# Row numbers read in place, a tangent for the experts' weights, and one load of all weights copied by VectorE in the tail of a convolution, attention and mixture-of-experts kernel

## The chip, the cores and the metric

The kernel runs on one core of a Trainium2 chip. The time is the device time of one execution, in microseconds (us). The engines are PE (TensorE; PEld is its weight load), DVE (VectorE), ACT (ScalarE), POOL (GpSimd) and SP (SyncE, which here only issues DMAs). The sixteen DMA engines of the core are shared by all queues. PE, DVE and ACT run in an order that the program writes out; SP's and POOL's orders are made by the scheduler when the kernel is built.

## The reference

```python
# x: (8, 56, 56, 256), float32
h = relu(bn(einsum('nhwc,cd->nhwd', x, w1)));  h = relu(bn(conv3x3(h, w2)))   # 32 paths, 4 channels each
h = relu(bn(einsum('nhwd,dc->nhwc', h, w3)))
x = relu(sum over the 32 paths of h + x)
t = tokens(x)                                          # (8, 3136, 256)
u = layernorm(t);  k = v = headwise_layernorm(u)       # 8 heads of 32
t = t + u + u @ (k^T v / N)                            # linear attention, per image and head
u = layernorm(t)
p = softmax(u @ router_w.T);  w, e = top_k(p, 2);  w = w / w.sum()
t = t + u + sum over the two e of w_e * (gelu(u @ w1[e] + b1[e]) @ w2[e] + b2[e])   # 8 experts
```

With two experts chosen of which the logits differ by d, the weights w are 1 / (1 + exp(d)) and exp(d) / (1 + exp(d)).

## The kernel before

The 25088 tokens are cut into 56 chunks of 448 (7 chunks an image). The program has 65 slots. Slot s works on several chunks at once: the third convolution of chunk s, the first two of chunks s + 2 and s + 1, the end of chunk s - 1 (sum, transposes, norms, the image's key-value products), the attention of chunk s - 8, and the routing of chunks whose attention is done. Into this the tiles of the experts are mixed. From slot 57 on there is no convolution left: this, with the tiles that follow slot 64, is the tail. It begins near 2660 us.

- Routing (`route_steps`, groups of two chunks or one): the logits, the two best experts, `q` = the difference of their logits. POOL raises e to the power q (L1110, `ebase` holds e), DVE makes the two weights from it with an add and a reciprocal (L1148 to L1154) and writes them, with the token's number, into the three last columns of its row (`pay`, 259 wide). A matmul with a triangle (L1119, L1125) ranks the tokens of an expert; the rank plus `count` (L1131), plus the first row of the expert, `offs` (L1135), is the row in DRAM (`regions`). POOL scatters 112 rows with one indirect DMA (L1165).
- Planning (`plan_steps`, L1227 to L1322): after certain chunks, `count` tells how many full tiles of 256 rows each expert has; a table holds the first row and the expert of every tile.
- Tiles (`moe_steps`, 210 of them, each one expert and 256 rows): `take_rows` reads the row number from the table into a register of SP and loads 256 rows (L1359, 259 KB); `take_weights` does the same with the expert and loads its weights (`w`, 513 KB, L1369) from `Wd` in DRAM; `tile_in` transposes the rows (L1380, `te`) and copies the tokens' numbers into a small tile `index` (L1389; for the 30 tiles that may be partial L1392 and L1393 mask them first); `tile_mid` is the first product (L1420) and the gelu (L1424), `tile_out` the second (L1436, L1440) and the scaling (L1444, into `y`); `tile_add` lets POOL add 128 rows of `y` to the output in DRAM with an indirect DMA (L1458, two a tile, 420 in all). Step n of the loop holds the first stage of tile n, the middle of tile n - 1, the last of tile n - 2, the loads of rows n + 2 and of weights n + 1.
- Buffers: `rows` 5, `w` 4, `index` 6, `y` 4. A buffer of `y` and of `index` comes free when the add that reads it has landed.
- Adds are ordered by block: a token's two experts are handled in two halves of a round (`blocks`), and the first add of a half waits until all adds of the half before have landed.
- The end of a chunk: DVE adds the paths' sum, the bias and the input (L688) into a buffer `u`; ACT applies relu (L717); it is stored (L722) and transposed (L729), and the transposed copy is stored (L734). In the convolution, DVE splits `h2` into `hi` (L343) and `lo` (L344), which are spread by DMA (L350).

Of the kernel before, what the change touches and what calls it, by code (L numbers as in the profile page):

```python
# [8 lines left out]
F32 = mybir.dt.float32  # L9
# [16 lines left out]
def kernel(  # L26
# [68 lines left out]
    xtp = ctx.enter_context(tc.tile_pool(name="xtp", bufs=4))  # L95
    taps = ctx.enter_context(tc.tile_pool(name="taps", bufs=1))
    split = ctx.enter_context(tc.tile_pool(name="split", bufs=1))
    hlp = ctx.enter_context(tc.tile_pool(name="hlp", bufs=2))
# [34 lines left out]
    ebase = const.tile([P, 2 * KT], F32, name="ebase")  # L133
    nc.gpsimd.memset(ebase, 2.718281828459045)
# [183 lines left out]
    def conv2_steps(s):  # L318
# [19 lines left out]
        def halves():  # L338

            h2 = h2s[s]  # L340
            hi = split.tile([P, CH], F32R, tag="hi", name=f"hi_{s}")
            lo = split.tile([P, CH], F32R, tag="lo", name=f"lo_{s}")
            nc.vector.tensor_copy(hi, h2)  # L343
            ins = nc.vector.tensor_tensor(lo, h2, hi.bitcast(F32), ALU.subtract).ins  # L344
            if s == 0:
                halved.append(ins)
            hl = hlp.tile([P, NQ, CH], F32R, tag="hl", name=f"hl_{s}")
            for v, part in enumerate((hi, lo, hi, lo)):
                queue = nc.scalar if s == 0 and v % 2 else nc.sync
                queue.dma_start(out=hl[v : P : 4, :, :].bitcast(F32), in_=part.bitcast(F32))  # L350
            h2s[s] = hl
# [220 lines left out]
    offs = const.tile([P, M], F32, name="offs")  # L572
    code = const.tile([P, M], F32, name="code")
    for e in range(M):
        nc.gpsimd.memset(offs[:, e : e + 1], float(0 if e == 2 * E else e % E * CAPR + TR))
        nc.gpsimd.memset(code[:, e : e + 1], float(E - e % E))
# [18 lines left out]
    nc.vector.memset(count, 0.0)  # L595
    nc.vector.memset(taken, 0.0)
# [77 lines left out]
    def sum_paths(s, u):  # L674
# [10 lines left out]
        if ab == NQ - 1:  # L685
            if f == 0:
                usum[s] = one.tile([P, NF, CH], F32, tag="u", name=f"u_{s}")
# [373 lines left out]
    def route_steps(group):  # L1061
# [42 lines left out]
        def weights():  # L1104
# [5 lines left out]
            nc.gpsimd.tensor_tensor(q, ebase[:T, :K], q, ALU.pow)  # L1110
# [3 lines left out]
        def ranks():  # L1114
# [20 lines left out]
            nc.vector.tensor_add(at, at, offs[:T, None, None, :E].to_broadcast([T, K, 2, E]))  # L1135
# [9 lines left out]
        def rows():  # L1145
            q2 = v["q"]
            q1 = small([], "rq1")
            nc.vector.tensor_scalar_add(q1, q2, 1.0)  # L1148
            nc.vector.reciprocal(q1, q1)
            for n, m in enumerate(group):  # L1150
# [3 lines left out]
                nc.vector.tensor_mul(pay[:, :, C + 1], q2[:, mine], q1[:, mine])  # L1154
# [36 lines left out]
    def plan_steps(b):  # L1191
# [63 lines left out]
        def runs():  # L1255
# [10 lines left out]
            nc.vector.scalar_tensor_tensor(  # L1266
                start, start, float(TR), offs[:, None, :m].to_broadcast([P, 2, m]),
                op0=ALU.mult, op1=ALU.add
            )
# [60 lines left out]
    def entry(i, j, most):  # L1330
# [3 lines left out]
            place[0:1, j : j + 1], engines=[mybir.EngineType.SP],  # L1334
# [3 lines left out]
        if b not in landed:  # L1338
# [5 lines left out]
    def empty_rows(e):  # L1344
        pad = slots.tile([P, 2, ROW], F32, tag="rows", name=f"pad_{e}", bufs=5)
# [9 lines left out]
    def take_rows(i):  # L1355
        row = entry(i, 0, E * CAPR - TR)
        z = slots.tile([P, 2, ROW], F32, tag="rows", name=f"rows_{i}", bufs=5)
# [8 lines left out]
    def take_weights(i):  # L1366
        e = entry(i, 1, E - 1)
        w = slots.tile([P, WROW], F32, tag="w", name=f"w_{i}")
# [5 lines left out]
    def tile_in(i):  # L1374
# [11 lines left out]
        index = slots.tile([P, 2], I32, tag="index", name=f"index_{i}", bufs=6)  # L1386
        low = slot_of[i][3]
        if low is None:
            nc.vector.tensor_copy(index, z[:, :, C + 2].bitcast(I32))  # L1389
        else:  # L1390
# [4 lines left out]
            )  # L1395
        turned[i] = (eT, g, index)
# [49 lines left out]

    blocks = {}

    def tile_add():
# [5 lines left out]
        at = bass.IndirectOffsetOnAxis(ap=index[:, h : h + 1], axis=0)  # L1455
# [91 lines left out]
    for s in range(S + A + 1):  # L1547
# [56 lines left out]
        if s == S + 1:  # L1604
            apart.append(s)
# [63 lines left out]
```

## Time and profile before

| | |
|---|---|
| median of three runs | 3119.7 us (3117.6 to 3120.1) |
| profiled execution | 3117.4 us, of which the span of the profile is 3115.6 |
| PE busy | 2889.5 us, 93% |
| DVE busy | 2175.9 us, 70% |
| ACT busy | 1915.0 us, 61% |
| POOL busy | 1850.0 us, 59% |
| DMA | 537.5 MB, 173 GB/s over the span |
| weight loads (L1369) | 210 of 513 KB |
| adds (L1458) | 420, 1575 ns of POOL each |
| powers on POOL for the experts' weights (L1110) | 32, 52.9 us busy |
| index copies (L1389) | 180, 338 ns each |

The page of the profile divides the span into 40 slices and gives each engine's busy share in tenths, the clock that PE was granted and the share of the DMA engines. A row of a group reads: line, engine, operation, output and inputs, how many, busy time and mean duration, and the idle time of the engine before them with what ended it. Waits are inferred from semaphores; one for several things is put down to the last of them.

### The profile page before, as it was taken

Reading aid. Unit: us, or ns where it says so; the run is one execution under the profiler, and the core shown is the slowest. Engines: PE = TensorE matmul, PEld = TensorE weight load, DVE = VectorE, ACT = ScalarE, POOL = GpSimd, SP = SyncE. Lnnn points to the kernel's source line nnn. Section 1 sums busy time; section 2 is a strip of 40 time slices with the busy share of each in tenths; the row PEclk is TensorE's granted clock in tenths of the full one; section 3 lists DMA queues with packets and bytes.
Section 4 is the critical chain, followed back from the end, with each engine's and each line's share of the span. In section 5 each row is a group of like instructions: output and inputs, shape, how many; then the busy total and the mean of one; then the engine's idle time right before and its main releaser. Section 6 shows DMA issues by size and latency. Waiting matters only on the chain.

```text
span 3115.6 us, 53761 instructions
## 1 busy us (share of the span) xinstructions
PE 2889.5 (93%) x16677; PEld 1648.9 (53%) x16677; DVE 2175.9 (70%) x5743; ACT 1915.0 (61%) x3827; POOL 1850.0 (59%) x1375
## 2 busy tenths in 40 slices
PE   7999889888899999999999999999999997997898
PEld 3334434333455555555555555555555554776777
DVE  6778788788777887787877787787778885543100
ACT  4666566556666666667666666666666664554345
POOL 2332355445465766656766666676664656677677
PEclk9999999899999999999999999999999998998999
DMA  3434344435566767676766776767766666998897
GB/s 106 145 117 130 114 147 123 133 108 178 142 165 184 197 170 193 172 191 194 187 192 163 196 198 170 193 171 196 196 170 173 186 165 153 221 263 208 199 219 177
DMA packets 321710, 537.54 MB, mean 173 GB/s; under 512 B 40192, under 2 KB 231824, under 8 KB 321424
## 3 DMA queue, kind: packets, MB, share of 16 engines
q1 hardware_dynamic: 238464, 429.89, 45.1%
q0 software_dynamic: 82368, 103.47, 18.3%
q8 instruction: 133, 2.18, 0.3%
q14 instruction: 153, 1.25, 0.1%
q10 hardware_dynamic: 592, 0.76, 0.1%
HBM read 248.01 MB, written 192.55 MB: 141 GB/s over the span
## 4 chain that ended last, share of the span: by engine, by line
PE 70%; DVE 10%; ACT 6%; issue 5%; DMA 4%; POOL 4%; SPq 0%; POOLq 0%; DVEq 0%; ACTq 0%
PE c L660 14%; PE su L681 13%; PE ph L1420 10%; PE py L1440 8%; PE at L984 6%; PE c L326 4%; PE kv L830 3%; DVE r L668 3%; ACT r L665 3%; PE te L1380 3%; DMA out_dram<-y,index 2%; PE c L290 2%; PE py L1436 2%; POOL hsd L794 2%; PE tu L729 1%
## 5 line engine op out<-in xcount | busy, mean ns | idle before, releaser
L668 DVE SCALAR_TENSOR_TENSOR r<-c,nb,r 128x448 f32<-128x448 f32 x1792 | 1127.0, 676 | 378.8 <-ACT r L665 376.5
L665 ACT ACTIVATE r<-c,b3t 128x448 f32<-128x448 f32 x1792 | 1038.2, 634 | 347.1 <-PE c L660 343.2
L1458 POOL DMA_INDIRECT out_dram<-y,index x420 | 661.3, 1575 | 327.3 <-ACT y L1444 185.2
L660 PE MATMUL c<-hl,W3hl 64*128 64x448 f32 x3584 | 689.6, 428 | 32.3 <-ACT r L665 19.0
L1165 POOL DMA_INDIRECT regions<-pay,rrowi x448 | 428.4, 956 | 316.2 <-PE c L660 194.7
L660 PEld LDWEIGHTS c<-hl,W3hl 64*128 64x128 f32 x3584 | 325.6, 188 | 494.4 <-issue 208.7
L681 PE MATMUL su<-r,gather 128*32 128x448 f32 x3584 | 535.4, 564 | 38.4 <-DVE r L668 34.3
L1444 ACT ACTIVATE y<-py,rows 128x256 f32<-128x256 f32 x420 | 196.1, 475 | 465.7 <-PE py L1440 363.8
L1420 PE MATMUL ph<-eT,w 128*128 128x256 f32 x1680 | 451.6, 400 | 29.2 <-ACT hT L1424 10.7
L1440 PE MATMUL py<-w,hT 128*128 128x256 f32 x1680 | 433.1, 382 | 1.7 <-ACT hT L1424 1.7
L1420 PEld LDWEIGHTS ph<-eT,w 128*128 128x128 f32 x1680 | 299.3, 193 | 162.6 <-issue 34.6
L794 POOL TENSOR_TENSOR hsd<-hsd,half 112x36 f32<-112x36 f32 x49 | 302.6, 6175 | 87.6 <-DVE hsd L792 85.8
L1440 PEld LDWEIGHTS py<-w,hT 128*128 128x128 f32 x1680 | 292.1, 192 | 31.6 <-ACT hT L1424 2.1
L1424 ACT ACTIVATE hT<-ph,w 128x256 f32<-128x256 f32 x420 | 197.4, 479 | 173.2 <-PE ph L1420 116.7
L984 PE MATMUL at<-tab,tT 128*112 128x272 f32 x896 | 259.3, 413 | 9.7 <-ACT r L665 6.6
L755 POOL TENSOR_TENSOR norm<-t,hmean 112x512 f32<-112x512 f32 x112 | 117.1, 1085 | 212.9 <-ACT r L665 101.9
L681 PEld LDWEIGHTS su<-r,gather 128*32 128x32 f32 x3584 | 97.6, 109 | 223.4 <-DVE r L668 102.4
L1436 PE MATMUL py<-b2hl,own 128*128 128x256 f32 x420 | 182.0, 433 | 16.2 <-ACT lg L992 8.6
L984 PEld LDWEIGHTS at<-tab,tT 128*112 128x112 f32 x896 | 148.2, 179 | 84.3 <-issue 28.2
L1110 POOL TENSOR_TENSOR rq<-ebase,rq 112x8 f32<-112x8 f32 (+1 forms) x32 | 52.9, 1652 | 210.2 <-DVE rq L1109 209.2
L1436 PEld LDWEIGHTS py<-b2hl,own 128*128 128x128 f32 x420 | 80.2, 191 | 146.9 <-issue 47.6
L988 DVE SCALAR_TENSOR_TENSOR X<-at,rs,X 112x256 f32<-112x256 f32 x224 | 106.8, 477 | 68.0 <-PE at L984 67.7
(265 smaller groups left out, 3192.4 us busy)
## 6 DMA issues: line engine op xcount, KB each, us to landing
w<-Wd SPq DMA_DIRECT2D x210, 513.0 KB
rows<-regions SPq DMA_DIRECT2D x210, 259.0 KB
xi<-in_x_dram SPq DMA_DIRECT2D x56, 448.0 KB
hl<-hi SPq DMA_DIRECT2D x112, 224.0 KB
tTs<-u SPq DMA_DIRECT2D x56, 448.0 KB
ts<-t SPq DMA_DIRECT2D x56, 448.0 KB
tT<-tTs SPq DMA_DIRECT2D x56, 448.0 KB
X<-ts SPq DMA_DIRECT2D x56, 448.0 KB
```

Of the source, the lines that this page charges most:

```text
L660: product = nc.tensor.matmul(tiles[g][:, :CH], W3hl[rows, ab, cg, :], hl[rows, ab, :], start=True, stop=True)
L665: nc.scalar.activation(r, tiles[0][:, :CH], AF.Relu, bias=b3t[:, cg, 2 * ab : 2 * ab + 1])
L668: nc.vector.scalar_tensor_tensor(r, tiles[1][:, :CH], nb3[:, cg, 2 * ab + 1 : 2 * ab + 2], r, op0=ALU.max, op1=ALU.add,)
L681: nc.tensor.matmul(ps[32 * c4 : 32 * c4 + 32, :CH], gather, unit.pop((s, 4 * u + c4)), start=(ab == 0), stop=(ab == NQ - 1),)
L794: nc.gpsimd.tensor_tensor(sd, sd, half[:T, :].rearrange("q (k h) -> q k h", k=KT), ALU.pow)
L984: nc.tensor.matmul(ps, tT[:, f, k * T : (k + 1) * T], tables_of[b][:, f, :], start=(f == 0), stop=(f == NF - 1),)
L1165: ins = nc.gpsimd.indirect_dma_start(out=regions[n], out_offset=bass.IndirectOffsetOnAxis(ap=v["row_i"][:, (m - group[0]) * KT + k, n : n ...
L1420: nc.tensor.matmul(ps, w[:, f * C + hf * P : f * C + (hf + 1) * P], eT[:, f, :], start=(f == 0), stop=(f == NF - 1),)
L1424: nc.scalar.activation(hT[:, hf, :], ps, AF.Gelu, bias=w[:, 2 * NF * C + hf : 2 * NF * C + hf + 1])
L1436: nc.tensor.matmul(ps, own.to_broadcast([P, P]), b2hl, start=True, stop=False)
L1440: nc.tensor.matmul(ps, hT[:, f, h * P : (h + 1) * P], w[:, (NF + f) * C : (NF + f + 1) * C], start=False, stop=(f == NF - 1),)
L1458: ins = nc.gpsimd.indirect_dma_start(out=out_rows, out_offset=at, in_=y[:, h, :], in_offset=None, compute_op=ALU.add, **partial,).ins
```

## The change

Six things are changed together.

1. The token numbers are no longer copied for full tiles: the indirect DMA reads them in the row tile itself. The rows' buffers go from 5 to 8, and the `index` buffers of the partial tiles from 6 to 12.
2. `count` and `taken` start from the first rows of the experts, so that `offs` is added neither to each token's row nor to each plan.
3. The experts' weights come from tanh(q/2) on ACT, as 0.5 + 0.5 tanh and 0.5 - 0.5 tanh; the power on POOL and the reciprocal on DVE go.
4. When the convolution is over (slot 57), its buffers are given up, and in their place one DMA loads the weights of all eight experts (`experts`, 4.2 MB). From then on `take_weights` reads the expert's number into a register of DVE, and DVE copies 128x1026 numbers into `w`. That concerns 80 of the 210 tiles.
5. For the room, the convolution's pools lie on the other side of the memory, `lo` takes the place of `h2`, and the sum of the paths that of `xT` instead of `u`.
6. The memsets of `ebase` and of half of `offs` go.

```diff
-    xtp = ctx.enter_context(tc.tile_pool(name="xtp", bufs=4))
...
+    conv_pools = [
+        tc.tile_pool(name=name, bufs=bufs, side="right")
+        for name, bufs in (("xtp", 4), ("taps", 1), ("split", 1), ("hlp", 2))
+    ]
+    xtp, taps, split, hlp = (p.__enter__() for p in conv_pools)
...
-            lo = split.tile([P, CH], F32R, tag="lo", name=f"lo_{s}")
             nc.vector.tensor_copy(hi, h2)
+            lo = h2.bitcast(F32R)
...
-    nc.vector.memset(count, 0.0)
-    nc.vector.memset(taken, 0.0)
+    for k in range(2):
+        nc.vector.tensor_copy(count[:, k], offs[:, :E])
+    nc.vector.tensor_scalar_mul(taken, count, 1.0 / TR)
...
-            if f == 0:
-                usum[s] = one.tile([P, NF, CH], F32, tag="u", name=f"u_{s}")
+            usum[s] = xTs[s]
...
-            nc.gpsimd.tensor_tensor(q, ebase[:T, :K], q, ALU.pow)
             both = v["both"] = small([2, E], "rboth", BF16)
...
-            nc.vector.tensor_add(at, at, offs[:T, None, None, :E].to_broadcast([T, K, 2, E]))
+            nc.scalar.activation(v["q"], v["q"], AF.Tanh, scale=0.5)
...
-            nc.vector.tensor_scalar_add(q1, q2, 1.0)
-            nc.vector.reciprocal(q1, q1)
+            nc.vector.tensor_scalar(q1, q2, -0.5, 0.5, ALU.mult, ALU.add)
+            nc.vector.tensor_scalar(q2, q2, 0.5, 0.5, ALU.mult, ALU.add)
...
-                nc.vector.tensor_mul(pay[:, :, C + 1], q2[:, mine], q1[:, mine])
+                nc.vector.tensor_copy(pay[:, :, C + 1], q2[:, mine])
...
-            nc.vector.scalar_tensor_tensor(
-                start, start, float(TR), offs[:, None, :m].to_broadcast([P, 2, m]),
-                op0=ALU.mult, op1=ALU.add
-            )
+            nc.vector.tensor_scalar_mul(start, start, float(TR))
...
-        z = slots.tile([P, 2, ROW], F32, tag="rows", name=f"rows_{i}", bufs=5)
+        z = slots.tile([P, 2, ROW], F32, tag="rows", name=f"rows_{i}", bufs=8)
...
     def take_weights(i):
+        w = slots.tile([P, WROW], F32, tag="w", name=f"w_{i}")
+        if apart:
+            e = entry(i, 1, E - 1, mybir.EngineType.DVE)
+            nc.vector.tensor_copy(
+                w, experts[0][:, bass.ds(e, 1), :].rearrange("q e c -> q (e c)")
+            )
+            weights_of[i] = w
+            return
         e = entry(i, 1, E - 1)
-        w = slots.tile([P, WROW], F32, tag="w", name=f"w_{i}")
         nc.sync.dma_start(
...
-        index = slots.tile([P, 2], I32, tag="index", name=f"index_{i}", bufs=6)
+        index = [z[:, h, C + 2 :].bitcast(I32) for h in range(2)]
         low = slot_of[i][3]
-        if low is None:
-            nc.vector.tensor_copy(index, z[:, :, C + 2].bitcast(I32))
-        else:
+        if low is not None:
+            index = slots.tile([P, 2], I32, tag="index", name=f"index_{i}", bufs=12)
...
-        at = bass.IndirectOffsetOnAxis(ap=index[:, h : h + 1], axis=0)
+        at = bass.IndirectOffsetOnAxis(ap=index[h], axis=0)
...
         if s == S + 1:
+            for pool in reversed(conv_pools):
+                pool.__exit__(None, None, None)
+            stay = ctx.enter_context(tc.tile_pool(name="stay", bufs=1, side="right"))
+            experts.append(stay.tile([P, E, WROW], F32, name="experts"))
+            nc.sync.dma_start(out=experts[0], in_=Wd.rearrange("e p c -> p e c"))
             apart.append(s)
```

More of the change, by code (lines that the diff above doesn't have):

```diff
@@ L93, in load @@
         xs_in[s] = X
-    xtp = ctx.enter_context(tc.tile_pool(name="xtp", bufs=4))
-    taps = ctx.enter_context(tc.tile_pool(name="taps", bufs=1))
-    split = ctx.enter_context(tc.tile_pool(name="split", bufs=1))
-    hlp = ctx.enter_context(tc.tile_pool(name="hlp", bufs=2))
+    conv_pools = [
[3 more added lines that the diff above has]
+    xtp, taps, split, hlp = (p.__enter__() for p in conv_pools)
     setup_pool = tc.tile_pool(name="setup", bufs=1)
@@ L132 @@
     nc.gpsimd.memset(half, 0.5)
-    ebase = const.tile([P, 2 * KT], F32, name="ebase")
-    nc.gpsimd.memset(ebase, 2.718281828459045)
     desc = const.tile([P, E], F32, name="desc")
@@ L571 @@
     nc.vector.tensor_copy(iot, iot_i)
-    offs = const.tile([P, M], F32, name="offs")
+    offs = const.tile([P, E], F32, name="offs")
     code = const.tile([P, M], F32, name="code")
+    for e in range(E):
+        nc.gpsimd.memset(offs[:, e : e + 1], float(e * CAPR + TR))
     for e in range(M):
-        nc.gpsimd.memset(offs[:, e : e + 1], float(0 if e == 2 * E else e % E * CAPR + TR))
         nc.gpsimd.memset(code[:, e : e + 1], float(E - e % E))
@@ L1328, with entry @@
     landed = set()
-    def entry(i, j, most):
+    def entry(i, j, most, engine=mybir.EngineType.SP):
         place, own, k, partial, b = slot_of[i]
         loads, (value,) = nc.values_load_multi_w_load_instructions(
-            place[0:1, j : j + 1], engines=[mybir.EngineType.SP],
+            place[0:1, j : j + 1], engines=[engine],
             min_val=0, max_val=most,
@@ L1337, in entry @@
         )
-        if b not in landed:
+        if b not in landed and engine == mybir.EngineType.SP:
             landed.add(b)
@@ L1344, in empty_rows @@
     def empty_rows(e):
-        pad = slots.tile([P, 2, ROW], F32, tag="rows", name=f"pad_{e}", bufs=5)
+        pad = slots.tile([P, 2, ROW], F32, tag="rows", name=f"pad_{e}", bufs=8)
         nc.gpsimd.memset(pad, 0.0)
@@ L1395, in tile_in @@
             )
+            index = [index[:, h : h + 1] for h in range(2)]
         turned[i] = (eT, g, index)
@@ L1445, in tile_out @@
         ready.append((i, h))
+    experts = []
     blocks = {}
```

## The prediction

> **What bounds the kernel now.** I read the page first, then the busy time of each engine by stretches, then the waits of the last 400 us, the chain of waits from 2560 us on, and last the timeline, for the gaps of PE and of POOL one by one.
>
> The page's slices show two stages. This line is PE in 40 slices of 78 us, then DVE, then the DMA engines:
>
> ```profile
> PE   7999889888899999999999999999999997997898
> ...
> DVE  6778788788777887787877787787778885543100
> ...
> DMA  3434344435566767676766776767766666998897
> ```
>
> From slice 12 to 33 PE is full and nothing else is. In the last six slices PE drops to 7 to 9, DVE goes idle, and the DMA engines are full. Stretches of the busy-time view (us, then busy of PE, its loads, DVE, ACT, POOL; granted clock, DMA share, GB/s) put numbers on it:
>
> ```profile
> 900.00:2590.00 1690.00, 1647.40 (x9849) 908.06 (x9850) 1322.01 (x3382) 1124.09 (x2254) 1092.72 (x764) 1.00 0.68 183
> 2640.00:3003.00 363.00, 309.03 (x1567) 259.92 (x1565) 124.52 (x589) 166.76 (x394) 258.57 (x192) 0.95 0.90 221
> 3003.00:3116.00 113.00, 100.36 (x530) 88.78 (x530) 7.70 (x45) 60.53 (x123) 85.39 (x56) 0.96 0.78 192
> ```
>
> The middle is PE-bound (97.5%, clock 1.00): nothing that frees another engine can give much there. In the last stretch the matmuls run one tile per 4.13 us without gaps. So the case is decided in 2640 to 3003. There PE idles 54 us (the timeline's gaps) at a clock of 0.95. POOL is busy 258.6 us, with 0.3 us between one indirect DMA and the next, 51 us in all: only 53 us of POOL are real gaps. PE and POOL are thus both some 85% taken, and DMA 90%. Who waits, from 2700 on (total us, times, longest):
>
> ```profile
> DVE index L1389 <- DMA out_dram<-y,index: 108.8, 21, 11.2
> DVE index L1393 <- DMA out_dram<-y,index: 97.5, 24, 8.6
> ACT y L1444 <- DMA out_dram<-y,index: 85.5, 18, 10.3
> ...
> DVE rq L1148 <- POOL rq L1110: 23.8, 3, 16.1
> ...
> PE ph L1420 <- DMA w<-Wd: 9.7, 8, 1.8
> ```
>
> Everything hangs on the adding DMAs (L1458) landing: a y buffer is free again only then. The chain from 2560 on says it in shares of those 556 us:
>
> ```profile
> by line: PE ph L1420 16.7%; PE py L1440 15.0%; DMA out_dram<-y,index 13.7%; issue 7.3%; POOL out_dram L1458 5.1%; DMA w<-Wd 4.8%; PE te L1380 3.7%; DMA regions<-pay,rrowi 3.4%; PE at L984 3.1%; POOL regions L1165 3.0%; PE py L1436 2.4%; ACT
> ```
>
> 76 us of the chain are adds in flight and 27 us weight loads in flight. Of 80.3 MB moved in 2640 to 3003, 61 weight loads are 61 x 0.525 = 32 MB.
>
> **The change, part by part.** Base: the profiled execution, 3117.4 us (span 3115.6); the median of the runs is 2.3 us above it.
>
> *Weights in the tail.* The instruction order of the changed kernel has 80 weight loads fewer on SP and 80 copies (128x1026) with a register load each on DVE. On DMA 42 MB go and 4.2 MB come. In 2640 to 3003 about 58 of the 61 loads go: 30 of 80 MB, DMA share 0.90 to about 0.60. Two gains:
> (a) The nine PE gaps ended by "DMA w<-Wd" sum to 9.7 us. They go: -9.7.
> (b) The adds land sooner. Their median is 5.8 us in 2640 to 3003, the fastest 3.7; 4.2 is my estimate at 60% load. Ten PE gaps there (2758 to 2987, 25 us in all) end with a y that waited for an add. Each shortened by 1.6 us or its own length: -13.8. From below, if the landing is the fixed latency of an add and not load: 0 (the middle, at DMA share 0.68, also shows 5.8, which speaks for this); from above the whole 25. I take half of the worked figure, -8, because of that middle row.
>
> *The copy's price on DVE.* Nearest row: the cast hi (L343), 128x448, 390 ns, against 167 for two elements, so 0.5 ns an element: 0.69 us a copy. At L344's pace (626 ns for 448) it is 1.23. The register load: SP's take 277 ns median, 1469 at most. So 1.0 to 2.7 us a tile, I take 1.2. DVE is busy 124 of 363 us: hidden. The copy is issued one and a half tiles (6 us) ahead of its matmul. It waits for PE's last read of the buffer four tiles back; behind it on DVE are the attention's X (L988), the routing and the plan, which wait for later PE work anyway: 0.
>
> *The copy's price on POOL.* The cast row:
>
> ```profile
> L343 DVE CAST hi<-h 128x448 fp32r<-128x448 f32 x56 | 21.9, 390 | 15.8 <-ACT h L335 15.7
> ```
>
> [...]The Trainium skill, "SBUF — State Buffer", section "SBUF: two separate sides", says against this change that an fp32 copy from SBUF to SBUF runs in a mode that locks GpSimd out of a shared port, and that descriptors of GpSimd's DMAs can't be written meanwhile. By that rule each copy could stop POOL for its 0.69 us: 58 x 0.69 = 40 us on the engine with 53 us of gaps, and the gain would be gone. In the trace, three adds overlap such a cast by up to 0.39 us and take 1.60 us, against a median of 1.56; the 79 adds that overlap an index copy average 1.585 against 1.572. I take 0.03 us a copy, 2 us in all, and keep 40 for the rival.
>
> *Loading all weights (4.2 MB).* SP issues it behind the stores of chunk 55 (L722, L734, at 2607 and 2609), and it waits for the first of them to land, until about 2612. At the 272 GB/s of 2700 to 2750 it takes 15 us, at the 168 of 2600 to 2650 25 us. Queued behind are the rows and weights of 2614 and 2621; their matmuls come at 2637 and after, because PE stands for 8.3 us until 2630 behind POOL's norm (L755) in any case. I take +3, between 0 and +15.
>
> *Token numbers in place.* 180 index copies (338 ns mean, 60.8 us busy) and their 109 us of waits for adds go. What waited behind them: the routing at 2867.6 stood for 6.7 us behind one, and PE's rank matmul with it (gap 9.98 us at 2870; after the like gap of 8.3 us at 2622 four matmuls took 2.08 us instead of 1.03, so 2 us more for the clock): -6.8 - 2 = -8.8. The other index waits end with the same add that y waits for; y is late next, so nothing more. With 8 instead of 5 row buffers a row load now waits for the adds of six tiles back; y_n-2 needs the same adds at the same step, and a row load has two steps (8.3 us) for its 3.6 us landing: 0. The 30 partial tiles keep their index, with 12 buffers.
>
> *Tanh in place of the power.* On POOL 32 powers (52.9 us, 1.65 each) go, 5 of them (9 us) in 2640 to 3003: POOL had 16 us of adds before one of them while DVE stood (DVE rq L1148). That delayed the scatters, not PE: gap 1.0 us. -2. On ACT 32 small activations, like lg's 172 ns: 5.5 us on an engine 62% busy; each waits for q (L1109), which is ready before the rank matmul's own input: 0. The skill, "ScalarE: Activation LUTs", section "Table sets: the hidden batching unit", has tanh listed in other sets than gelu: with this trace's 1283 ns a load and two loads a group, 32 x 2.6 = 82 us of ACT. But the changed kernel's ACT order has two table loads, as before: 0.
>
> *Counts from the first rows, and the small edits.* 32 adds of offs (27.9 us; 931 ns mean, stretched by the power beside them) go, a reciprocal becomes a tensor_scalar. In the middle, sixteen short PE gaps (0.2 to 0.9 us) follow a stretched L1135 or index copy, some 7 us in all. They mostly go: -4. The buffers dropped (lo, u) and the pools moved move no instruction on PE: 0.
>
> *Sum.* -9.7 - 8 - 8.8 - 2 + 2 + 3 - 4 = -27.5. Is there room? PE at full clock needs about 300 us of the 363, POOL 310 - 10 = 300: the tail may become 337 and both still wait for each other, 89% full. So 3117.4 - 27.5 = 3090, and with the 2 us to the median about 3092.
>
> **The rivals.**
> *1. POOL is already the bound (3109).* From 2846.7 to 2920.4 POOL works without a gap, and it stands only 53 us. If its queue sets the adds' time, only the powers (-9), the direct weight waits that it doesn't replace (-3) and the middle (-4) count, with the load's +3 and the lock's +2: -11, and the 2 us to the median. For it: adds and scatters at 1.85 and 1.25 us a piece need 3.7 us of the tile's 4.13. Against: POOL's gaps of 4.5 to 7.3 us, which end with a y that PE delivered late.
> *2. Everything clears (3068).* The adds land in 3.7 us, all 25 us of y gaps go, and PE's clock stays at 1.00 (8 us more): -27.5 - 17 - 8 = -52, and the 2 us.
> *3. Slower: the copies lock POOL out (3135).* Place: POOL's indirect DMAs from 2660 to the end. POOL's 300 us in 2640 to 3003 become 300 + 58c with c the POOL time that a copy costs. Half of its 53 us of gaps stay, since the first add of a block waits until the block before has landed. So it decides from 300 + 26 + 58c = 363, c = 0.64 us, on: just what the rule gives for 0.69 us copies (366), and 398 at 1.23. The mean of the two is 19 us over 363; with the middle's 4 off, +15, and the 2 us to the median. PE's gains are void then, as y waits for POOL. Against it stand the three overlaps above.
> *4. The edit does nothing that shows (3117):* the landing is latency, and the freed waits end on y.
>
> **How the numbers follow.** The forecast and its near surroundings (3075 to 3105) have 0.58, rival 2 0.12, rival 1 0.15, rival 4 0.06, rival 3 0.09. The likeliest gives 3092. The range 3066 to 3116 leaves out most of rivals 3 and 4 and the far side of 2. A measurement here tells apart about 0.2%, 6 us. Faster by more: 0.85; within: 0.06; slower: 0.09.
>
> **What would show it.** Right: in the tail no wait of DVE or PE for w or index, DMA share near 0.6, adds landing near 4.5 us, copies of 0.7 us, L1458 still at 1.56 to 1.6 us with 0.3 between, PE busy over 88% from 2640 until 4.13 us a tile sets in. Wrong: L1458 or its spacing stretched to over 2 us (rival 3); POOL without gaps while y waits (rival 1); landing still 5.8 us; PE idle for over 10 us at 2615 to 2640 behind the 4.2 MB.

## The result and the profile after

The changed kernel takes 3098.3 us (median of four runs, 3096.96 to 3099.31) against 3118.64 us of the kernel before (four runs, 3115.54 to 3120.09): the ratio is 0.9937, with a 95% interval of 0.9922 to 0.9952. The execution with the profile took 3097.54 us, span 3095.8. So the kernel is 20 us faster. The forecast was 26 us faster, and its time lies 6 us from the measured one. But the gain was not made where the forecast put it, and the experiments show that part 4, the largest part of the forecast, made the kernel slower.

Three marks can be read in every trace: ACT's relu (L717) of chunk 20, that of chunk 55, and the end of the span. They cut the execution into a start, a middle and a tail. (The tail by these marks begins at 2605.9 us in the kernel before, some 54 us ahead of slot 57.)

| us | start | middle | tail | span |
|---|---|---|---|---|
| before | 883.2 | 1722.7 | 509.7 | 3115.6 |
| changed | 877.7 | 1704.7 | 513.4 | 3095.8 |

Of the prediction's -27.5 us, -4 was to come from the middle and -23.5 from the tail. The middle gave -18.0, the start -5.5, and the tail became 3.7 us longer.

The slices of the page after (PE, DVE and the DMA engines in 40 slices) show the tail changed as intended in DMA, and not in PE:

```profile
PE   7999889888999999999999999999999997997897
...
DVE  6878787788777777786777777787778783654221
...
DMA  3534344436566767677676776767666667766664
```

The DMA engines, at 8 or 9 tenths in five of the last six slices before, stand at 6 or 7 and end with 4. PE has the same 7 to 9. The busy-time view for the two stretches of the tail that the prediction showed (us, then busy of PE, its loads, DVE, ACT, POOL; granted clock, DMA share, GB/s), and for the middle of before and of after, between the marks:

```profile
2640.00:3003.00 363.00, 318.77 (x1614) 272.13 (x1613) 155.10 (x575) 175.47 (x410) 263.46 (x188) 0.93 0.69 135
3003.00:3096.00 93.00, 73.97 (x391) 65.12 (x389) 14.97 (x45) 41.85 (x89) 72.27 (x44) 0.92 0.40 66
...
883.20:2605.90 1722.70, 1673.71 (x10013) 922.90 (x10011) 1348.02 (x3474) 1139.02 (x2283) 1104.66 (x772) 0.99 0.68 182
877.70:2582.40 1704.70, 1662.11 (x10012) 919.19 (x10011) 1306.35 (x3336) 1140.14 (x2303) 1071.47 (x751) 1.00 0.69 184
```

First two rows: the DMA share of the first stretch fell from 0.90 to 0.69, where the prediction had 0.60, and that of the second from 0.78 to 0.40. Last two rows: the middle has the same 10012 matmuls, and PE's idle time fell from 49.0 to 42.6 us (the stretch less PE's busy time), while PE's busy time fell by 11.6 us. DVE lost 41.7 us of work, POOL 33.2.

The waits of PE from 2640 us on show what took the place of the waits for weights:

```profile
PE te L1383 <- DMA rows<-regions: 16.7, 9, 4.9
PE py L1439 <- ACT lg L992: 10.3, 1, 10.3
PE rk L1118 <- DVE rboth L1111: 6.2, 2, 5.5
```

The 9.7 us for `w` are gone. In their place, PE's first transposes of a tile wait 16.7 us for rows, which the prediction had costed at 0. And POOL now ends late. In the kernel before, the last `y` (3105.2) is 3.4 us ahead of the last add (3108.6); in the changed kernel it is 10.8 us ahead (3077.9 and 3088.7), with a queue of adds behind it. (These are starting times.) The operation view by shape, from 2640 us on, has the reason in its mean durations (busy us, mean ns of one; the first line is of before, the others of after):

```profile
L1458 POOL DMA_INDIRECT out_dram<-y,index x175 | 273.0, 1560 | 105.0 <-issue 30.3 <-ACT y L1444 28.5 <-ACT hT L1424 12.8
...
L1462 POOL DMA_INDIRECT out_dram<-y,rows x107 | 171.9, 1606 | 75.7 <-ACT y L1447 24.2 <-issue 15.9 <-ACT lg L992 11.1
L1462 POOL DMA_INDIRECT out_dram<-y,index x60 | 100.6, 1677 | 18.3 <-ACT hT L1427 5.8 <-issue 5.2 <-DVE index L1395 3.0
L1366 DVE COPY w<-experts 128x1026 f32 x80 | 57.0, 714 | 149.9 <-PE py L1443 113.5 <-PE te L1383 6.8 <-ACT y L1447 5.8
```

An add took 1.56 us and takes 1.61 to 1.68. The timeline of POOL and DVE near the end points to the copies (start, duration):

```profile
3044.12 1.55 POOL L1462 DMA_INDIRECT out_dram<-y,index  x1 [0.30 <-issue]
3045.98 1.92 POOL L1462 DMA_INDIRECT out_dram<-y,index  x1 [0.31 <-ACT hT L1427]
...
3047.11 0.70 DVE L1366 COPY w<-experts 128x1026 f32 x1 [3.05 <-PE py L1443]
```

The add without a copy beside it takes 1.55 us, the one with a copy 1.92. From 2640 us to the end, 59 adds overlap a copy and average 1.776 us (at most 2.09), 107 do not and average 1.553; from one add to the next it is 2.08 us against 1.86. The 20 scatters (L1164) that overlap a copy take 1.13 us, the other 44 take 0.95. From 2960 us on, most adds beside a copy (16 of 26) have the next one 2.2 to 2.3 us behind them, where the others have 1.85. Two adds a tile, one of each kind, then make 4.12 us, and PE delivers a tile every 4.13 us. So the queue that POOL has by then is not worked off: the adds stay 8 to 11 us behind their `y` from 2975 us to the end, where in the kernel before they catch up to 0.3 us. It is paid at the end.

### The profile page after: what moved, and what is told of

Same layout as the page of the kernel before. It is cut to its first block, busy times and chain, and to the rows that moved or that the text cites. A ratio compares the mean times of both kernels' runs of the same rounds, so it can differ in the third digit from the quotient of the medians.

```text
span 3095.8 us, 53406 instructions
## 1 busy us (share of the span) xinstructions
PE 2876.5 (93%) x16677; PEld 1645.7 (53%) x16677; DVE 2179.3 (70%) x5612; ACT 1917.4 (62%) x3859; POOL 1815.3 (59%) x1333
## 4 chain that ended last, share of the span: by engine, by line
PE 68%; DVE 9%; POOL 7%; ACT 6%; issue 5%; DMA 4%; SPq 0%; POOLq 0%; DVEq 0%; ACTq 0%
PE c L661 14%; PE su L682 13%; PE ph L1423 10%; PE py L1443 8%; PE at L984 6%; PE kv L830 3%; ACT r L666 3%; PE c L325 3%; POOL hsd L794 3%; PE te L1383 3%; DVE r L669 3%; PE c L289 2%; DMA out_dram<-y,rows 2%; PE py L1439 2%; POOL out_dram L1462 2%
## 5 line engine op out<-in xcount | busy, mean ns | idle before, releaser
L1462 POOL DMA_INDIRECT out_dram<-y,rows x360 | 571.8, 1588 | 407.0 <-ACT y L1447 270.5
L1164 POOL DMA_INDIRECT regions<-pay,rrowi x448 | 431.7, 964 | 308.6 <-PE c L661 166.4
L1439 PE MATMUL py<-b2hl,own 128*128 128x256 f32 x420 | 181.8, 433 | 14.3 <-ACT lg L992 10.3
L1366 DVE COPY w<-experts 128x1026 f32 x80 | 57.0, 714 | 149.9 <-PE py L1443 113.5
```

Of the source, the lines that this page charges most:

```text
L1164: ins = nc.gpsimd.indirect_dma_start(out=regions[n], out_offset=bass.IndirectOffsetOnAxis(ap=v["row_i"][:, (m - group[0]) * KT + k, n : n ...
L1439: nc.tensor.matmul(ps, own.to_broadcast([P, P]), b2hl, start=True, stop=False)
L1462: ins = nc.gpsimd.indirect_dma_start(out=out_rows, out_offset=at, in_=y[:, h, :], in_offset=None, compute_op=ALU.add, **partial,).ins
```

## Experiments

Each run was timed against the kernel before on its own chip. On the chip of the first four, before had a median of 3133.95 us (3119.60 to 3141.51); on that of the second four 3127.47, and 3124.16 on the same chip later, for `e9` to `e11`; for `e12`, on another, 3122.13. The ratio is of all runs of a kernel to those of before on its chip, and is not quite that of the medians. The times are from one trace a kernel, and the runs of one kernel differ by up to 22 us (52 runs of before on one chip), so a few us in one trace are no finding by themselves. On the chip of `e1` to `e4` no trace of before was taken. All profiles cut by the same marks:

| us | ratio (95%) | start | middle | tail | span |
|---|---|---|---|---|---|
| before, again (`e9`) | | 895.3 | 1722.3 | 509.6 | 3127.2 |
| `e1` without the load and copies | 0.9907 (0.9885 to 0.9929) | 880.5 | 1709.0 | 514.2 | 3103.7 |
| `e2` index in place alone | 0.9983 (0.9972 to 0.9994) | 884.6 | 1718.9 | 524.4 | 3127.9 |
| `e3` tanh alone | 0.9965 (0.9948 to 0.9982) | 876.6 | 1720.5 | 519.2 | 3116.3 |
| `e4` counts alone | 0.9957 (0.9947 to 0.9968) | 887.9 | 1715.7 | 517.0 | 3120.6 |
| `e5` changed, again | 0.9951 (0.9938 to 0.9963) | 880.6 | 1709.3 | 516.8 | 3106.7 |
| `e6` copies by ScalarE | 0.9889 (0.9873 to 0.9904) | 882.5 | 1706.9 | 500.1 | 3089.5 |
| `e7` copies in a slow form on VectorE | 0.9917 (0.9904 to 0.9931) | 878.6 | 1712.1 | 513.2 | 3103.9 |
| `e8` no load, 14 row buffers | 0.9909 (0.9896 to 0.9922) | 878.7 | 1706.6 | 515.8 | 3101.1 |
| `e10` ScalarE, then slow form | 0.9860 (0.9838 to 0.9883) | 877.7 | 1708.9 | 494.3 | 3080.9 |
| `e11` ScalarE, 10 row buffers | 0.9875 (0.9853 to 0.9896) | 876.1 | 1704.2 | 497.1 | 3077.4 |
| `e12` both of these | 0.9889 (0.9869 to 0.9909) | 880.4 | 1703.8 | 497.6 | 3081.8 |

### The parts one by one

`e1` is the changed kernel without the 4.2 MB load and the 80 copies; the weights of each tile come by DMA as before.

```diff
     def take_weights(i):
-        if apart:
+        if False:
...
```

> The changed kernel with its part 4 undone: every tile's weights come by DMA from DRAM, as before; all else as changed. Theory A (from the two traces): the change earned its time before slot 57 (the last key-value sum stands at 2632.4 us against 2656.9), and its tail is no faster, as DVE's copies stretch POOL's adds from 1.55 to about 1.97 us. Then this kernel keeps the 24 us of the middle, has adds of 1.55 to 1.6 us, PE gaps for w of some 10 us again, and 3093 to 3101 us in all. Rival B (the prediction): the loads out of the tail are worth 18 us less 5 for price; then 3109 to 3114 us.

Measured: 3104.46 us, ratio 0.9907. The tail is 514.2 us, within 3 us of the changed kernel's 513.4 and 516.8. So the load and the copies, for which 42 MB of DMA traffic went, gain nothing. The ratio is even lower than the changed kernel's (0.9937, and 0.9951 for `e5`), which speaks for a loss; `e8` takes this up.

`e2` is the index read in place alone, with the buffers that pay for it (7 row buffers fit).

```diff
-        index = slots.tile([P, 2], I32, tag="index", name=f"index_{i}", bufs=6)
+        index = [z[:, h, C + 2 :].bitcast(I32) for h in range(2)]
```

> The kernel before with the token numbers read in place alone (part 1, and the buffers of part 5 for the room; 7 row buffers instead of 8). Theory A: the index copies in the middle stand behind POOL's operations (338 ns on average instead of 167, up to 2.9 us) and hold up the convolution; without them the last key-value sum comes 8 to 15 us earlier, and the time is 3100 to 3108. Rival B (the prediction): only the tail gains, 9 us; the last key-value sum moves by under 3 us, the time is 3107 to 3111.

Measured: 3127.12 us, ratio 0.9983. Its middle is 3.8 us shorter than that of the first profile of before, its tail 14.7 us longer, of which up to 10.5 go with the clock: 38.6 us of full clock are missing in it, against 28.1 (how this is counted stands under `e9`). From 2640 us on DVE's index of the partial tiles stands for rows, and PE for weights:

```profile
DVE index L1391 <- DMA rows<-regions: 162.1, 26, 53.4
...
PE ph L1419 <- DMA w<-Wd: 13.0, 8, 2.7
```

Before, the same wait of DVE (L1393) was 17.5 us. That a row buffer kept until the tile's adds have landed delays the next load into it fits this; `e11` takes it up. By all its runs `e2` is still 0.17% faster than before, so the longer tail of this trace is no loss that the runs confirm.

`e3` is the tangent alone, `e4` the counts from the first rows alone.

```diff
-            nc.gpsimd.tensor_tensor(q, ebase[:T, :K], q, ALU.pow)
+            nc.scalar.activation(v["q"], v["q"], AF.Tanh, scale=0.5)
```

> The kernel before with tanh on ACT in place of the power on POOL alone (part 3). Theory A: the power holds up DVE's add of offs (931 ns instead of 290) and the wait for q (7.7 us in the middle); without it the last key-value sum comes 5 to 10 us earlier; 3106 to 3113. Rival B (the prediction): 2 us and a part of the middle's 4: 3114 to 3117. If tanh had to load a table each time it would be over 3140.

```diff
-            nc.vector.tensor_add(at, at, offs[:T, None, None, :E].to_broadcast([T, K, 2, E]))
```

> The kernel before with the counts starting from the first rows alone (part 2). Theory A: 32 adds go, 24 of them stretched to 931 ns by the power beside them; what stands behind them waits for the power's port then, or not at all: 2 to 5 us, 3112 to 3117. Rival B: under 2 us, not to be told from before.

Measured: 3118.17 us, ratio 0.9965, and 3120.47 us, ratio 0.9957. By the ratios, the three parts save 0.17, 0.35 and 0.43% of the time, 0.95% together, and `e1`, which has all three, saves 0.93%: the parts add up, within intervals of 0.1 to 0.2% each. In the middle of the traces, `e2`, `e3` and `e4` save 3.8, 2.2 and 7.0 us, and `e1` 13.7. But 1.8, 3.5 and 5.1 us of these, and 3.4 of `e1`'s, go with the clock, which differs by up to 7.0 us between traces with the same middle (3.0 us missing in `e8`, 10.0 in `e7`). What is left, 2.0, -1.3 and 1.9, does not make the 10.3 of `e1`; which part brings the rest is not resolved. In the operation view of DVE between the marks, the first two lines (of before) are gone in the changed kernel, and the last two are the same line of code in before and after:

```profile
L1389 DVE COPY index<-rows 128x2 int32<-128x2 int32 x116 | 47.4, 409 | 0.1
L1135 DVE TENSOR_TENSOR rrow<-rrow,offs 112x128 f32<-112x128 f32 x16 | 16.7, 1042 | 0.6
...
L1148 DVE TENSOR_SCALAR rq<-rq 112x8 f32<-112x8 f32 x16 | 2.8, 177 | 0.0
...
L1147 DVE TENSOR_SCALAR rq<-rq 112x8 f32<-112x8 f32 x16 | 10.5, 656 | 0.0
```

The add of `offs` took 1042 ns for what the add one line above it (L1131), of the same shape, did in 281. The prediction put this down to the power beside it on POOL. In `e3`, which has no power, the same 16 adds still take 902 ns on the mean. Without the add, the next operation of the group, 177 ns before, takes 656. So a stall stays and moves to the next operation on DVE; which instruction of POOL makes it was not tried.

### The copies and POOL

Four runs on one chip. `e5` is the changed kernel itself.

> The changed kernel itself, on the chip of the runs that follow, as their standard. Both theories: ratio to the kernel before 0.991 to 0.995 (0.9922 to 0.9952 was measured), the last y some 11 us ahead of the last add, the last adds of the tail 1.85 us on the mean beside VectorE's copies and 1.55 without.

Measured: 3112.89 us (3108.46 to 3117.91), ratio 0.9951. Its tail is like the first profile's: 61 adds beside a copy average 1.778 us, 109 others 1.555, and from add to add it is 2.10 us against 1.86. That is 0.22 to 0.24 us for each of some 60 adds, and with the scatters beside a copy some 16 us of POOL.

`e6` gives the copies to ScalarE, `e7` leaves them on VectorE in another form.

```diff
-            e = entry(i, 1, E - 1, mybir.EngineType.DVE)
-            nc.vector.tensor_copy(
+            e = entry(i, 1, E - 1, mybir.EngineType.Activation)
+            nc.scalar.copy(
```

> The changed kernel with the 80 copies of weights made by ScalarE instead of VectorE. Theory A (what stretches the adds is VectorE's copy holding the memory port it shares with POOL): every add of the tail takes 1.55 us, POOL gains 0.25 to 0.42 us a copy, 20 to 33 us in all, the backlog of 11 adds behind the last y is gone (last add within 4 us of the last y), and the kernel ends 8 us sooner than the changed kernel, unless ScalarE's 80 copies of about 1 us hold up hT and y (its busy share in the tail goes from 0.49 to about 0.70): then 0 to 5 us are left. Theory B (any engine that reads 0.5 MB and writes 0.5 MB of the on-chip memory per tile stretches the adds): adds beside a copy stay at 1.75 to 1.85 us, the backlog stays, and the time is that of the changed kernel or a few us more.

```diff
-            nc.vector.tensor_copy(
-                w, experts[0][:, bass.ds(e, 1), :].rearrange("q e c -> q (e c)")
+            nc.vector.tensor_reduce(
+                w, experts[0][:, bass.ds(e, 1), :].rearrange("q e c -> q c e"), AX.X, ALU.add
```

> The changed kernel with each copy of weights made on VectorE by a reduction over an axis of length one: the same engine, the same bytes, another operation, estimated at 1.2 us instead of 0.70 (twice the time per element). Theory A1 (the lock belongs to the fast form of the copy): the adds beside it are back at 1.55 us and the end comes 8 us sooner than with the changed kernel. Theory A2 (any large operation of VectorE holds the port): the adds beside it are stretched at least as much, for longer (0.5 us a copy and more, 40 us of POOL and more): POOL needs over 4.13 us a tile, and the end comes 5 to 20 us later than with the changed kernel.

Measured: 3093.56 us, ratio 0.9889, 19 us sooner than `e5`; and 3102.93 us, ratio 0.9917, 10 us sooner. The copies and the two kinds of adds from 2640 us on, in `e5`, `e6` and `e7` in this order:

```profile
L1366 DVE COPY w<-experts 128x1026 f32 x80 | 57.0, 713 | 149.2 <-PE py L1443 74.7 <-ACT y L1447 41.8 <-issue 9.2
L1462 POOL DMA_INDIRECT out_dram<-y,rows x110 | 177.5, 1614 | 81.2 <-ACT y L1447 40.8 <-issue 18.5 <-ACT lg L992 5.3
L1462 POOL DMA_INDIRECT out_dram<-y,index x60 | 100.5, 1674 | 18.3 <-ACT hT L1427 5.8 <-issue 4.9 <-DVE index L1395 4.6
...
L1366 ACT COPY w<-experts 128x1026 f32 x80 | 84.2, 1053 | 3.5 <-issue 2.8
L1462 POOL DMA_INDIRECT out_dram<-y,rows x110 | 171.7, 1560 | 79.2 <-ACT y L1447 29.0 <-issue 15.8 <-ACT hT L1427 9.6
L1462 POOL DMA_INDIRECT out_dram<-y,index x60 | 92.7, 1544 | 18.7 <-issue 7.0 <-ACT y L1447 4.6 <-ACT hT L1427 3.7
...
L1366 DVE TENSOR_REDUCE w<-experts 128x1026 f32 x80 | 97.4, 1222 | 128.5 <-PE py L1443 88.2 <-ACT y L1447 11.4 <-issue 9.7
L1462 POOL DMA_INDIRECT out_dram<-y,rows x110 | 171.0, 1554 | 93.6 <-ACT y L1447 41.5 <-issue 16.9 <-ACT hT L1427 14.7
L1462 POOL DMA_INDIRECT out_dram<-y,index x60 | 92.6, 1543 | 18.3 <-issue 8.2 <-ACT y L1447 3.7 <-ACT hT L1427 3.4
```

The adds are back at 1.54 to 1.56 us in both. In `e7` the same engine moves the same bytes between the same places, and 81 adds overlap such a copy: they average 1.547 us, the others 1.553. So neither the bytes nor VectorE as such stretch the adds, but the fast form of the copy (0.71 us against 1.22). The last `y` is 3.4 us ahead of the last add in both, as it was before: the queue at the end is gone. This fits the lock which the prediction weighed and priced at 0.03 us a copy. The busy-time view of the tails of `e5`, `e6`, `e7` and `e8` has POOL's price in its fifth busy time, 379.7 us against 362.4 to 364.6, and PE's gain in the first: it is busy for the same 437 to 438 us in all four, and idle for 79.5, 63.2, 76.1 and 77.5.

```profile
2589.90:3106.70 516.80, 437.28 (x2197) 369.51 (x2195) 188.79 (x678) 245.47 (x548) 379.65 (x266) 0.94 0.66 134
2589.40:3089.50 500.10, 436.92 (x2196) 369.74 (x2195) 133.73 (x598) 314.06 (x628) 364.26 (x266) 0.93 0.68 139
2590.70:3103.90 513.20, 437.10 (x2196) 369.67 (x2195) 230.97 (x678) 247.80 (x548) 362.39 (x266) 0.93 0.67 135
2585.30:3101.10 515.80, 438.31 (x2196) 369.35 (x2195) 133.31 (x598) 243.93 (x548) 364.59 (x266) 0.93 0.84 208
```

`e7` gains less than `e6`. It loses time while VectorE still has the routing of the last chunks: from tile 140's transposed rows (`eT`, L1387) to tile 150's it takes 66.5 us, `e5` 58.6 and `e6` 57.9. That its longer copies hold the routing up is argued from this. From tile 160 on, when routing is over, it is the quickest of the three: 230.0 us to tile 209, against 240.4 and 234.6.

`e8` is again without the load and the copies, with the experts' room given to row buffers in the tail.

```diff
+        if late:
+            z = late[0].tile([P, 2, ROW], F32, tag="late", name=f"rows_{i}", bufs=14)
...
```

> The changed kernel without the load of all weights and without the copies (each tile's weights come by DMA as in the kernel before); the memory that the experts' weights took goes to 14 row buffers for the tail instead of 8. Theory A (the weights' traffic on the DMA engines is what holds the tail; row buffers don't matter): as without part 4, 0.9907 of the kernel before. Theory B (there the tail lost to tiles whose rows came late, VectorE's index waiting 148 us for rows): with more row buffers the loads start earlier, that wait falls to under 40 us, the tail gains 8 to 12 us on that, 0.987 to 0.988 of the kernel before, faster than the changed kernel.

Measured: 3100.38 us, ratio 0.9909, as `e1`. DVE's index waits still stand at 173 us, and the tail is 515.8. Where the weights come by DMA (DMA share 0.90 from 2640 to 3000), more row buffers buy nothing.

On the same chip the changed kernel itself (`e5`) is 12.5 us slower, and the intervals of the two ratios, 0.9896 to 0.9922 and 0.9938 to 0.9963, lie apart. The row buffers aside, the two differ by the load and the copies. `e1`, with eight row buffers, has the same ratio as `e8`. So part 4, with VectorE's fast copies, costs more than it brings: without it the kernel is faster. With ScalarE's copies (`e6`) it brings 6.8 us over `e8`, by intervals that overlap slightly. The traces show only 5.6 of the 12.5 us, and 1.0 of it in the tail: they hold the slowest of `e8`'s five runs and the fastest of `e5`'s six. Where the rest lies is not shown.

### The middle, and versions that beat both

`e9` is the kernel before once more.

> The kernel before itself, once more with a profile, so that the middle (from the relu of chunk 20 to that of chunk 55) and the tail (from there to the last add) can be set against the experiments' profiles taken on other chips than the first. Theory A (the changed kernel's gain is made in the middle): the middle takes 1721 to 1725 us, as in the first profile (1722.7), against 1705 to 1709 in the changed kernel, and the tail 501 to 504 us, against 506 to 510. Rival: the middle differs between chips, and is within 3 us of 1709 here; then the gain of the middle was the chip's.

Measured: one execution, 3128.89 us. Middle and tail are within 0.4 us of the first profile of before. (The tail is taken to the span's end throughout, 7 us behind the start of the last add; the bounds written ahead for the tail are therefore 7 us lower.) The gain of the middle is the change's, not the chip's. The start is 12.1 us longer than in the first profile of the same code. The busy-time view of both starts:

```profile
0.00:883.20 883.20, 783.62 (x4471) 359.63 (x4472) 687.15 (x1610) 537.03 (x1002) 373.92 (x332) 0.94 0.44 132
0.00:895.30 895.30, 798.81 (x4471) 367.04 (x4472) 687.26 (x1610) 537.56 (x1003) 373.89 (x332) 0.92 0.43 130
```

The same 4471 matmuls, 99.6 us of PE idle against 96.5: the difference is in the granted clock, 0.94 against 0.92. By the clock record, 51 us of full clock are missing in the first and 73 in the second (half of the time at half clock). So the -5.5 us of the changed kernel's start are no gain that can be told from this spread.

The same sum for the middle is 10.2 us missing in before, 9.9 in `e9`, 4.7 in the changed kernel, 6.8 in `e5`; in `e7` and `e10`, whose middle has the same code, it is 10.0. One of the dips of before, in three windows and in PE's timeline:

```profile
1274.28:1277.69 3.41, 1.98 (x13) 1.24 (x12) 3.13 (x12) 2.33 (x5) 1.93 (x2) 1.00 1.08 329
1277.69:1281.10 3.41, 3.41 (x15) 1.85 (x15) 2.31 (x9) 0.47 (x1) 0.00 (x0) 0.50 1.02 367
1281.10:1284.52 3.42, 3.23 (x25) 2.10 (x17) 1.32 (x3) 1.75 (x4) 0.94 (x1) 1.00 0.79 182
...
1277.59 0.73 PE L901 MATMUL cs<-A,mean_of 128*128 128x128 f32 x2 [0.90 <-DVE A L894]
1278.32 1.91 PE L1420 MATMUL ph<-eT,w 128*128 128x256 f32 x4
```

PE waits 0.90 us for DVE, and in all 1.43 us of the first window. In the second the clock is 0.50, and its four matmuls take 1.91 us, where four take 1.03 to 1.13 at full clock (1700 to 1800 us). The windows are not chosen at will: in the clock record of each of the fourteen traces, every stretch at half clock begins on a grid of steps of 3.41 us that holds through the whole execution, and lasts a whole number of steps, up to the span's end. The grid lies elsewhere in each execution. Of the steps at full clock (without the first nine and the last three of a trace), all 197 in which PE was busy for less than 40% were followed by one at half clock, 178 of the 839 with 40 to 80%, and 2 of the 10823 with 80% or more. So how much PE works in such a step goes with the clock of the next, and a gap is the dearer when others fall into the same step.

The Trainium skill, "TensorE: Matmul & The Clock Gate", section "What's actually happening", has the clock fall to half after an idle window of about 3.4 us, watched by a window that runs freely. The grid agrees with the second. The first is too mild here: by it gaps of 0.8 to 2.3 us, the longest beside four of the dips of before, would cost no clock, and a step with PE busy for 58% did. A grid that lies elsewhere in each execution also fits the starts that differ; that it makes them differ was not tried by itself.

`e10` puts each kind of copy where it was best.

```diff
+            late = i >= 168
+            e = entry(i, 1, E - 1, mybir.EngineType.DVE if late else mybir.EngineType.Activation)
+            if late:
+                nc.vector.tensor_reduce(
...
+            else:
+                nc.scalar.copy(
```

> The copies of weights made by ScalarE for the tiles up to number 167, and by VectorE with the reduction over an axis of length one from 168 on. Theory A (ScalarE is the right place while VectorE still has the last chunks' routing, since there VectorE's 1.22 us copies cost PE 12 us; behind them ScalarE's copies hold up y and hT, and VectorE's slow form costs nothing): the first half of the tail as with ScalarE alone, the second as with the slow form alone (230 us from tile 160 to 209 instead of 235), 3 to 5 us sooner than with ScalarE alone, 0.987 to 0.988 of the kernel before. Theory B (tiles at the end are limited by adds and row loads, whatever makes the copies): the time of ScalarE's copies, 0.989.

Measured: 3082.05 us (3076.93 to 3082.77), ratio 0.9860. The tail is 494.3 us, 5.8 shorter than with ScalarE alone. From tile 160 to 209 it takes 233.9 us (234.6 with ScalarE alone), so the expected gain of that part did not come; the tail is shorter ahead of it, where both kernels have the same copies, and PE's idle time in it is no shorter (64.9 us, 63.2 with ScalarE alone). 25.3 us of clock are missing in it, against 35.0. The intervals of the two ratios overlap. The place for the two forms is thus not shown to matter.

`e11` has all copies by ScalarE and ten row buffers; for the room there are three buffers of weights, and eight `index` buffers of the partial tiles instead of twelve.

```diff
-        z = slots.tile([P, 2, ROW], F32, tag="rows", name=f"rows_{i}", bufs=8)
+        z = slots.tile([P, 2, ROW], F32, tag="rows", name=f"rows_{i}", bufs=10)
...
-        w = slots.tile([P, WROW], F32, tag="w", name=f"w_{i}")
+        w = slots.tile([P, WROW], F32, tag="w", name=f"w_{i}", bufs=3)
```

> All copies by ScalarE, with ten row buffers instead of eight; the room comes from the weights' buffers, three instead of four. Theory A (rows that come late because a row buffer is held until its tile's adds have landed cost PE 5.9 us in three gaps in the run with ScalarE's copies, 14 to 17 us with VectorE's): these gaps are gone, and the end comes 3 to 6 us sooner than with eight buffers, 0.987 to 0.988 of the kernel before. Theory B (the fourth buffer of weights is needed more): PE waits for ScalarE's copies at the first product of a tile, no gain or up to 10 us lost.

Measured: 3084.57 us (3079.6 to 3085.21), ratio 0.9875; tail 497.1 us, 3.0 shorter than in `e6`. PE has no wait for rows in the tail any more; between 2850 and 2950 its gaps of 0.4 to 3.6 us in the same places now end on ACT's `y` or `eT`. So with eight row buffers PE does wait for rows, and with ten the next wait stands close behind: PE's idle time in the tail is 67.2 us, not shorter than `e6`'s 63.2, and what is shorter is again the time at the lower clock (25.1 us missing against 35.0).

`e12` has both edits.

> The two edits that gained most, together: ScalarE copies the weights up to tile 167, VectorE's slow form from 168 on, and ten row buffers with three buffers of weights. Theory A (they act on different waits: the copies' place, and the row buffers that are held): PE's waits for rows in the hybrid, 15.7 us in nine gaps, mostly go, the tail is 3 to 8 us shorter than the hybrid's 487, and the kernel is at 0.983 to 0.985 of the kernel before. Theory B (with one fewer buffer of weights VectorE's slow copies, 1.2 us each, come late for PE): as the hybrid or up to 5 us worse, 0.986 to 0.988.

Measured: 3085.32 us, ratio 0.9889. The two edits do not add up: the tail is 497.6 us, PE's waits for rows are gone, and gaps that end on `y` have taken their place. The intervals of `e10`, `e11` and `e12` overlap, so which of the three is the best stays open. All three have a ratio whose interval lies below that of the changed kernel, and on the chip of `e5`, `e10` and `e11` the medians are 28 and 31 us under it (3084.57 and 3082.05, against 3112.89).

## Why the prediction was right, and where it was not

The sign and the size were right, but the size by luck: the middle gave 14 us more than was foretold and the tail 27 us less, and the start 5.5 us that cannot be told from its spread. Part 4, the largest part of the forecast, was a loss.

- *"The middle ... nothing that frees another engine can give much there", -4.* This is the step that failed in the gain's favour. It read a stretch that is 97.5% PE as one that other engines can't shorten, and counted only the sixteen gaps that follow a stretched operation. Measured: -18.0, and -10.6 to -16.1 in the six other traces with the same middle (`e1`, `e5` to `e8`, `e10`). Of the 18.0, 6.4 are PE's idle time, 5.5 clock, and the other 6.1 are shorter busy time of the same matmuls. Idle time (42.3 to 44.8 us in these traces, 49.0 before) and busy time without the lost clock (1656.5 to 1658.9, 1663.4 before) hold from trace to trace; the clock part does not (3.0 to 10.0 us missing, 10.2 and 9.9 before). So the gaps were sized about right, and what the term put at nothing is PE's busy time, 5 to 7 us. Why it is shorter may be short waits inside the groups; that is not resolved.
- *The copy's price on POOL, "0.03 us a copy, 2 us in all".* This step failed on the other side. Measured: 0.22 us for each of some 60 adds and 0.16 to 0.18 us for each of 15 to 20 scatters, 16 to 17 us of POOL, and 0.42 us for most of the adds beside a copy in the last stretch. Of the forecast's own signs of being wrong, a spacing of over 2 us came true for these adds. The Trainium skill, "SBUF — State Buffer", section "SBUF: two separate sides", had the direction right, and `e7` shows that of the two forms only the fast one does it. The 40 us that the prediction worked out from it, a full stop of POOL for each copy's 0.69 us, were too much; the row taken instead, three adds that overlapped a 0.39 us cast, was too small a sample. Rival 3 needed 0.64 us a copy to make the whole kernel slower than before, and the measured price stays under that; but it was enough to make part 4 a loss (`e8`).
- *"A row load has two steps for its 3.6 us landing: 0".* Measured: 16.7 us of PE waits for rows (14.4 in `e5`), gone with ten buffers in `e11`.
- *(a), -9.7.* The waits for weights are gone, as said. *(b), -8.* An add's median landing in the tail is 4.1 us with its index in the row tile, where it was 5.8. That the lower DMA load did this is not shown, since the median fell in the middle too, where the DMA share was 0.68 and is 0.69 (the view of DMA issues from 900 to 2590 us, before and changed):

```profile
out_dram<-y,index POOLq DMA_INDIRECT x230, 5.8
...
out_dram<-y,rows POOLq DMA_INDIRECT x230, 4.9
```

The stretched adds and the late rows took the place of the waits that went. What the load and the copies are worth where the copies don't stretch the adds: in the traces the tail of `e6` is 14.1 us shorter than that of `e1` and 15.7 shorter than that of `e8`, where (a), (b) and the load's +3 make -14.7; by the medians of all runs `e6` is only 6.8 us ahead of `e8`. So the terms were of the right size at best, and about twice too large by the medians. Against before, the shortest tail of all (`e10`) is 15.4 us shorter, out of the 23.5 foretold.
- *Slips in the sums.* The waits for `w` are eight, not nine, and half of 13.8 is 6.9, not 8. Neither changes the forecast by more than 1 us.
- *Token numbers in place, -8.8.* The gap of PE's rank matmul fell from 9.98 to 5.46 us, about half of what was foretold. Alone (`e2`), the edit comes with a tail 14.7 us longer, 10.5 of it clock.
- *Tanh, -2, and no table loads.* The trace of the changed kernel has two table loads (1283 ns each), as before. The middle gained 2.2 us in `e3`, by the clock alone.
- *Loading all weights, +3.* No PE gap between 2590 and 2640 us is new; the one of 8.2 us there was 8.3 before. The term is not seen.

What stays open: the tails of `e1` to `e4` are 4.5 to 14.7 us longer than those of the two profiles of before, which are from other chips, also with `e3` and `e4`, whose edits hardly touch it. The clock sum goes with most of it: behind chunk 55 it is 30.1, 38.6, 34.3 and 35.0 us missing in `e1` to `e4`, against 28.1 and 26.1 in the two profiles of before. Whether the edits, the chip or the place of the grid makes the dips there was not tried. Nor do the traces say where most of the 29 us lie that parts 1 to 3 save by the ratio of `e1`: its middle shows 13.7 of them.

## What to carry to other kernels

When work is moved to an idle engine, ask what that engine shares with the one that limits the stretch, and measure the operation's form too: here the same copy cost POOL 16 to 17 us on VectorE in its fast form and nothing in a slower form or on ScalarE. A stretch in which PE is 97% busy can still give time: here its idle time gave 4 to 7 us and its busy time, clock aside, 5 to 7 more. And a buffer that is kept longer needs its price taken from the loads that refill it: compare the tail before and after by the same marks, since the total can be right for the wrong reasons. Then leave each part out and time several runs: one trace of each hid more than half of the 12.5 us that part 4 cost.

## What was not expected of the hardware

- VectorE's copy of 128x1026 f32 in 0.71 us lengthens POOL's indirect DMA beside it from 1.55 to as much as 2.09 us. As a reduction over an axis of length one, 1.22 us, it leaves it at 1.54 to 1.55 us. ScalarE's copy takes 1.05 us and leaves it at 1.54 to 1.56.
- Two executions of the same code differ by 12.1 us in the first 900 us with the same matmuls and about the same PE idle time, at a granted clock of 0.94 and 0.92.
- The clock changes on a grid of 3.41 us that lies elsewhere in each execution. A step in which PE is busy for less than 40% is followed by one at half clock (197 of 197), one with 80% or more almost never (2 of 10823).
